# Edge-gated graph layer: a float32r expansion of two exact parts, masks and a subtraction on GpSimd, and lists built between edge tiles

## Chip, cores and metric

One core of a Trainium2 chip. The metric is the device time of one execution in microseconds (us), as a median over several. The profile shows one execution: TensorE (PE, with PEld for its weight loads), VectorE (DVE), ScalarE (ACT), GpSimd (POOL) and SyncE (SP, which only issues DMAs here). A ratio of two kernels is the mean time of one kernel's runs over the mean of the other's runs of the same rounds, so it is not quite the ratio of the medians that are quoted.

## The reference

16 batches, 1024 nodes, 256 features, everything in fp32. The adjacency matrix has some 9 entries in a column, so only these edges are worked on.

```
pre_u = x @ W1[:256];  pre_v = x @ W1[256:]
S[b,u,v] = sigmoid(relu(pre_u[b,u] + pre_v[b,v] + b1) @ W2 + b2)      # one gate per edge
a[b,v]   = sum_u S[b,u,v] * A[u,v] * x[b,u]
m[b,v]   = (sum_u A[u,v] * x[b,u]) * x[b,v]
z        = beta1*x + beta2*(a @ Wa + ba) + beta3*(m @ Wm + bm)
```

## The kernel before

The batches go in 4 **groups** of 4. A **block** is 128 target nodes of one group: 8 blocks to a group, 32 in all. Each block has two **windows** of 64 nodes, each window 640 edge slots in five **edge steps** of 128. `lists` makes, once per 128 nodes, which slot holds which edge. `rows` makes pre_u (written to a table in HBM) and pre_v (`pv`, kept in SBUF) for the next group.

```python
# lists(vt), its end: edge values fetched, then the masks (64 columns per edge step)
for j in range(TW):                      # 5 indirect DMAs for each of two windows
    nc.gpsimd.indirect_dma_start(out=val[:, i, j:j + 1], in_=adj_flat, in_offset=... vidx ...)
for j in range(TW):
    nc.vector.tensor_scalar(whose[:, i, j, :], place, L[:, j, 4:5], val[:, i, j:j + 1],
                            ALU.is_equal, ALU.mult)

# edges(g, vt, pv): one edge step j of window w
f = fetched[n % NF]                      # NF = 5 buffers
nc.gpsimd.indirect_dma_start(out=f, in_=table[g], in_offset=... uidx[:, i, j:j + 1] ...)
pc = psc.tile([P, 2, 2 * D], FP)         # PSUM, two buffers: the expansion of pre_v to slots
for h in range(2):
    q = (w + h) % 2 * W
    nc.tensor.matmul(pc[:, h, :], mark[q:q + W, j * P:(j + 1) * P], pv[q:q + W, h, :], ...)
nc.vector.tensor_tensor(t, f[:, :GD], pc, ALU.add)
for b in range(GB):                      # relu, times W2, summed: one score per edge and batch
    nc.vector.scalar_tensor_tensor(t[:, b, :], t[:, b, :], 0.0, w2_b, ALU.max, ALU.mult, accum_out=sc[:, b:b + 1])
nc.scalar.activation(gt, sc, AF.Sigmoid, bias=b2_b)
left = wk.tile([P, GB, 2, W], FP, name="left")            # three buffers
nc.scalar.activation(left[:, :, w, :], whose[:, i, j, :] (4 times), AF.Copy)         # ungated half
for b in range(GB):
    nc.scalar.activation(left[:, b, 1 - w, :], whose[:, i, j, :], AF.Copy, scale=gt[:, b:b + 1])
for b in range(GB):
    nc.tensor.matmul(acc[:, b, :], left[:, b], f[:, GD + b * D:GD + (b + 1) * D], ...)  # accumulation

# the main program
copy_h(0)
for nt in range(NT):
    pvs.append(rows(0, nt))
    lists(nt)                            # all eight lists before the first edge
for g in range(NG):
    for vt in range(NT):
        edges(g, vt, now[vt])
        if g + 1 < NG: pvs.append(rows(g + 1, vt))
```

A scheduler puts these instructions in order on each engine; within an engine they then run strictly in that order.

Of the kernel before, what the change touches and what calls it, by code (L numbers as in the profile page):

```python
# [8 lines left out]
FP = mybir.dt.float32  # L9
I32 = mybir.dt.int32  # L10
# [3 lines left out]
P = 128  # L14
# [3 lines left out]
def kernel(  # L18
# [18 lines left out]
):  # L37

# [54 lines left out]
    w_a = load_weights(Wa, "w_a")  # L93
    w_m = load_weights(Wm, "w_m")
    bias = load_rows(bm, D, "bias")
    ba_b = load_rows(ba, D, "ba_b")
    be1 = load_rows(beta1, 1, "be1")
    be2 = load_rows(beta2, 1, "be2")
    be3 = load_rows(beta3, 1, "be3")
    nc.vector.tensor_scalar(ba_b, ba_b, be2, None, ALU.mult)  # L100
    nc.vector.scalar_tensor_tensor(bias, bias, be3, ba_b, ALU.mult, ALU.add)
    nc.vector.tensor_scalar(w_a, w_a, be2, None, ALU.mult)
    nc.vector.tensor_scalar(w_m, w_m, be3, None, ALU.mult)
# [21 lines left out]
    nc.vector.tensor_scalar(before, row_of.rearrange("p w t v -> p w (t v)"), row, None, ALU.is_gt)  # L125
    late = const.tile([P, 1], FP, name="late")
# [10 lines left out]
    whose = const.tile([P, NT * NW, TW, W], FP, name="whose")  # L137
    thr = const.tile([P, NT], FP, name="thr")
    rest = const.tile([P, NT], FP, name="rest")
    nc.vector.memset(val, 0.0)  # L140
# [4 lines left out]
    pvp = main.enter_context(tc.tile_pool(name="pvp", bufs=NT + 1))  # L145
    wk = main.enter_context(tc.tile_pool(name="wk", bufs=3))
# [8 lines left out]
    def lists(vt):  # L155
# [42 lines left out]
        for w in range(NW):  # L198
            i = vt * NW + w
            Rv = Rw[:, w * RC:(w + 1) * RC]  # L200
            first = Rw[:, NW * RC + w:NW * RC + w + 1]
            nc.vector.tensor_tensor(Rv[:, 0:1], Rv[:, 0:1], first, ALU.add)
            nc.vector.tensor_copy(Rv[:, 1:2], first)
            early = wk.tile([P, E], FP, name="early", bufs=1)
            nc.vector.tensor_scalar(early, slot, Rv[:, 0:1], None, ALU.is_lt)
            mark = big.tile([P, E], FP, name="mark")
            nc.vector.scalar_tensor_tensor(mark, slot, first, early, ALU.is_ge, ALU.mult)  # L207
            nc.sync.dma_start(who[i], mark)
            pe = small("pe")
            for j in range(TW):  # L210
                nc.tensor.matmul(pe[:, j * RC:(j + 1) * RC], mark[0:W, j * P:(j + 1) * P], Rv[0:W, :],  # L211
                                 start=True, stop=True)
            L = wk.tile([P, TW, RC], FP, name="L", bufs=2)
            nc.vector.tensor_copy(L, pe[:, :TW * RC].rearrange("p (j r) -> p j r", r=RC))
            s_of = wk.tile([P, TW], FP, name="s_of", bufs=2)
            nc.vector.tensor_tensor(s_of, slot_of, L[:, :, 1], ALU.subtract)
            eq = wk.tile([P, TW, S], FP, name="eq", bufs=2)
            nc.vector.tensor_tensor(eq, nth.unsqueeze(1).to_broadcast([P, TW, S]),
                                    s_of.unsqueeze(2).to_broadcast([P, TW, S]), ALU.is_equal)
            nc.vector.tensor_tensor(eq, eq, L[:, :, 5:], ALU.mult)  # L220
            k_of = wk.tile([P, TW], FP, name="k_of", bufs=2)
            nc.vector.tensor_reduce(k_of, eq, AX.X, ALU.add)  # L222
            nc.vector.tensor_scalar(uidx[:, i, :], k_of, -1.0, float(N), ALU.mult, ALU.add)
            nc.vector.tensor_tensor(k_of, L[:, :, 2], k_of, ALU.subtract)
            nc.vector.scalar_tensor_tensor(k_of, L[:, :, 3], -BIG, k_of, ALU.mult, ALU.add)
            nc.vector.tensor_scalar(vidx[:, i, :], k_of, BIG + N, None, ALU.add)
            for j in range(TW):
                nc.gpsimd.indirect_dma_start(  # L228
                    out=val[:, i, j:j + 1], out_offset=None, in_=adj_flat,
                    in_offset=bass.IndirectOffsetOnAxis(ap=vidx[:, i, j:j + 1], axis=0),  # L230
                    bounds_check=N * N - 1, oob_is_err=False)
            for j in range(TW):
                nc.vector.tensor_scalar(whose[:, i, j, :], place, L[:, j, 4:5], val[:, i, j:j + 1],
                                        ALU.is_equal, ALU.mult)




    def rows(g, nt):
        hT = big.tile([P, GB, DC, P], FP, name="hT")  # L240
        nc.sync.dma_start(hT.rearrange("p b c n -> p (b c) n"),
                          xT_rows[:, g * GB * DC:(g + 1) * GB * DC, nt * P:(nt + 1) * P])
        hs = wk.tile([P, 2, DC, P], FP, name="hs", bufs=2)
        for w in range(NW):
            nc.gpsimd.tensor_copy(hs[:, :, :, w * W:(w + 1) * W],
                                  hT[:, 2:4, :, (1 - w) * W:(2 - w) * W])
        tab = big.tile([P, GD], FP, name="tab")
        pv = pvp.tile([P, 2, 2 * D], FP, name="pv")
        for h in range(2):
            pu = small("pu")  # L250
            for bb in range(2):
                for c in range(DC):
                    nc.tensor.matmul(pu[:, bb * D:(bb + 1) * D], hT[:, 2 * h + bb, c, :], w_u[:, c, :],  # L253
                                     start=(c == 0), stop=(c == DC - 1))
            nc.scalar.copy(tab[:, 2 * h * D:(2 * h + 2) * D], pu)  # L255
            pp = small("pp")
            for bb in range(2):
                for c in range(DC):
                    left = hs[:, bb, c, :] if h else hT[:, bb, c, :]
                    nc.tensor.matmul(pp[:, bb * D:(bb + 1) * D], left, w_v[:, c, :],  # L260
                                     start=(c == 0), stop=(c == DC - 1))
            nc.vector.tensor_tensor(pv[:, h, :].rearrange("p (b d) -> p b d", b=2),  # L262
                                    pp.rearrange("p (b d) -> p b d", b=2),
                                    b1_b.unsqueeze(1).to_broadcast([P, 2, D]), ALU.add)
        nc.sync.dma_start(table[g][nt * P:(nt + 1) * P, :GD], tab)
        return pv

# [7 lines left out]
    for i in range(NF):  # L275
        t = gat.tile([P, 2 * GD], FP, name=f"fetched{i}")
        nc.vector.memset(t, 0.0)
# [3 lines left out]
    def edges(g, vt, pv):  # L281
# [3 lines left out]
        for w in range(NW):  # L285
            i = vt * NW + w
            mark = big.tile([P, E], FP, name="mark")
            nc.sync.dma_start(mark, who[i])
            acc = psa.tile([P, GB, D], FP, name="acc")
            for j in range(TW):  # L290
# [3 lines left out]
                gt = wk.tile([P, GB], FP, name="gt")  # L294
# [4 lines left out]
                pc = psc.tile([P, 2, 2 * D], FP, name="pc")  # L299
                for h in range(2):  # L300
                    q = (w + h) % 2 * W
                    nc.tensor.matmul(pc[:, h, :], mark[q:q + W, j * P:(j + 1) * P], pv[q:q + W, h, :],  # L302
                                     start=True, stop=True)
                t = big.tile([P, GB, D], FP, name="t")
                nc.vector.tensor_tensor(t, f[:, :GD].rearrange("p (b d) -> p b d", b=GB),  # L305
                                        pc.rearrange("p h (b d) -> p (h b) d", b=2), ALU.add)
                sc = wk.tile([P, GB], FP, name="sc")
                for b in range(GB):
                    nc.vector.scalar_tensor_tensor(t[:, b, :], t[:, b, :], 0.0, w2_b,  # L309
                                                   ALU.max, ALU.mult, accum_out=sc[:, b:b + 1])  # L310

                nc.scalar.activation(gt, sc, AF.Sigmoid, bias=b2_b)  # L312
                left = wk.tile([P, GB, 2, W], FP, name="left")
                nc.scalar.activation(left[:, :, w, :], whose[:, i, j, :].unsqueeze(1).to_broadcast([P, GB, W]), AF.Copy)  # L314
                for b in range(GB):
                    nc.scalar.activation(left[:, b, 1 - w, :], whose[:, i, j, :], AF.Copy, scale=gt[:, b:b + 1])  # L316
                for b in range(GB):
                    nc.tensor.matmul(acc[:, b, :], left[:, b].rearrange("p k v -> p (k v)"),  # L318
                                     f[:, GD + b * D:GD + (b + 1) * D],
                                     start=(j == 0 and b % 2 == 0), stop=(j == TW - 1), skip_group_check=True)  # L320
            ev = big.tile([P, GB, D], FP, name="ev")
# [3 lines left out]
            for q in range(2):  # L325
# [6 lines left out]
                nc.scalar.copy(LT[:, q * 4:q * 4 + 4, 1, w * W:(w + 1) * W], src[:, :, a0:a0 + W])  # L332
        z = big.tile([P, GB, D], FP, name="z")
# [12 lines left out]

    copy_h(0)
    pvs = []
    for nt in range(NT):
        pvs.append(rows(0, nt))  # L350
        lists(nt)
    for g in range(NG):
        if g + 1 < NG:
            copy_h(g + 1)
        now, pvs = pvs, []
        for vt in range(NT):
            edges(g, vt, now[vt])
            if g + 1 < NG:
                pvs.append(rows(g + 1, vt))
    main.close()  # L360


    longest = const.tile([P, NT], FP, name="longest")
    nc.gpsimd.partition_all_reduce(longest, rest, P, bass_isa.ReduceOp.max)
    most = const.tile([P, 1], FP, name="most")
    nc.vector.tensor_reduce(most, longest, AX.X, ALU.max)
    turns = const.tile([P, NT + 1], I32, name="turns")
    nc.vector.tensor_copy(turns[:, :NT], longest)
    nc.vector.tensor_copy(turns[:, NT:], most)
# [109 lines left out]
```

## Time and profile before

| | before |
|---|---|
| median | 1948.74 us (1943.71 to 1953.58, 3 runs; with a fourth, 1949.91) |
| first store of z | 327.7 us |
| block in groups 0, 1, 2 / in group 3 | 51.8 / 45.5 us |
| boundary between groups | 67.2 us |
| busy: TensorE / VectorE / GpSimd | 82% / 61% / 23% |

The rows on blocks are read from the timeline of the SyncE queue: each store of z ends one block, so the distance of two stores is a block, and the distance from the last store of a group to the first of the next is a boundary. Groups of instructions have the columns: line, engine, operation, shape, count | busy us, mean ns | idle us before it, what ended most of it.

```profile
L295 POOL DMA_INDIRECT fetched<-table,uidx x320 | 326.3, 1020 | 1195.4 <-PE acc L318 982.4
L309 DVE SCALAR_TENSOR_TENSOR t<-t,w_b 128x256 f32<-128x256 f32 x1280 | 471.2, 423 | 18.4 <-DVE t L305 0.5
```

GpSimd has almost nothing but the gathers to do, and waits in front of them for the accumulation that frees a buffer. A multiply takes 423 ns.

### The profile page before, as it was taken

The numbers are of one execution on the slowest core, as the hardware profiler recorded it, in microseconds if no ns is written. First come the engines' busy times: TensorE is split into PE (matmuls) and PEld (weight loads), VectorE is DVE, ScalarE is ACT, GpSimd is POOL, SyncE is SP. The second block draws the span as 40 slices with busy tenths as digits, with TensorE's granted clock in tenths as the row PEclk, the third lists the DMA queues.
The fourth block names the chain that finished last, engine by engine and source line by source line (L and its number), as shares of the span: only waits on it lengthen the run. The fifth ranks groups of instructions, "written<-read, shape, count | busy, mean of one in ns | idle before, by whom it ended". The sixth has DMA issues, their size and how long they took to land. (4 is left out here: it accounts for less than half of the span.)

```text
span 1944.6 us, 22106 instructions
## 1 busy us (share of the span) xinstructions
PE 1590.1 (82%) x6640; PEld 1116.4 (57%) x6640; DVE 1193.9 (61%) x3595; ACT 726.4 (37%) x2306; POOL 442.1 (23%) x479
## 2 busy tenths in 40 slices
PE   1456459998888879999888879999998878989996
PEld 1345436666666646666666646666666645566664
DVE  4566666766666546566666456565566456766664
ACT  0000014444444324444444334344444334454443
POOL 0243352122222121221222122212221121222220
PEclk9676579999999989999999989999999989999999
DMA  9722247666666466666666466666666376666662
GB/s 273 244 86 83 69 156 263 208 242 245 240 248 248 144 228 223 216 235 224 233 245 238 152 241 242 237 224 221 228 230 232 130 267 245 244 238 235 227 236 98
DMA packets 151809, 414.09 MB, mean 213 GB/s; under 512 B 16656, under 2 KB 100112, under 8 KB 115472
## 3 DMA queue, kind: packets, MB, share of 16 engines
q0 software_dynamic: 48640, 296.70, 42.7%
q1 hardware_dynamic: 100800, 114.31, 17.4%
q10 hardware_dynamic: 2240, 1.58, 0.4%
q8 instruction: 55, 0.90, 0.2%
q14 instruction: 74, 0.61, 0.1%
HBM read 412.66 MB, written 55.57 MB: 241 GB/s over the span
## 5 line engine op out<-in xcount | busy, mean ns | idle before, releaser
L318 PE MATMUL acc<-fetched,left 128*128 128x256 f32 x2560 | 623.1, 394 | 78.8 <-ACT left L316 78.0
L318 PEld LDWEIGHTS acc<-fetched,left 128*128 128x128 f32 x2560 | 483.0, 195 | 248.5 <-ACT left L316 179.0
L295 POOL DMA_INDIRECT fetched<-table,uidx x320 | 326.3, 1020 | 1195.4 <-PE acc L318 982.4
L305 DVE TENSOR_TENSOR t<-fetched,pc 128x1024 f32<-128x1024 f32 x320 | 383.5, 1216 | 318.0 <-PE pc L302 285.9
L309 DVE SCALAR_TENSOR_TENSOR t<-t,w_b 128x256 f32<-128x256 f32 x1280 | 471.2, 423 | 18.4 <-DVE t L305 0.5
L302 PE MATMUL pc<-pv,mark 64*128 64x512 f32 x1280 | 404.2, 636 | 66.3 <-DVE t L305 59.7
L316 ACT ACTIVATE left<-whose,gt 128x64 f32<-128x64 f32 x1280 | 347.6, 339 | 9.5
L302 PEld LDWEIGHTS pc<-pv,mark 64*128 64x128 f32 x1280 | 130.3, 189 | 246.9 <-issue 119.7
L314 ACT ACTIVATE left<-whose 128x256 f32<-128x256 f32 x320 | 132.6, 414 | 367.4 <-PE acc L318 351.5
L312 ACT ACTIVATE gt<-sc,b_b 128x4 f32<-128x4 f32 x320 | 94.3, 295 | 322.1 <-DVE t L309 289.5
L255 ACT COPY tab<-misc 128x512 f32<-128x512 f32 x64 | 37.4, 585 | 400.4 <-PE misc L253 400.4
L253 PE MATMUL misc<-w_u,hT 128*128 128x256 f32 x512 | 135.7, 413 | 24.4 <-DMA hT<-in_xT_dram 24.4
L341 PE MATMUL misc<-w_m,LT 128*128 128x256 f32 x512 | 138.5, 394 | 1.7 <-ACT LT L332 0.3
L343 DVE TENSOR_TENSOR z<-misc,z 128x512 f32<-128x512 f32 x64 | 44.3, 692 | 153.5 <-PE misc L341 153.5
L341 PE MATMUL misc<-w_a,LT 128*128 128x256 f32 x512 | 132.7, 382 | 0.0
L253 PEld LDWEIGHTS misc<-w_u,hT 128*128 128x128 f32 x512 | 105.3, 208 | 40.6 <-DMA h_blk<-in_adjT_dram 24.4
L329 PEld LDWEIGHTS misc<-ident,ev 128*128 128x128 f32 x512 | 55.8, 142 | 103.3 <-ACT ev L324 103.3
L262 DVE TENSOR_TENSOR pv<-misc,b_b 128x512 f32<-128x512 f32 x64 | 44.1, 689 | 114.8 <-PE misc L260 113.3
L211 PE MATMUL misc<-Rw,mark 64*128 64x29 f32 x160 | 36.9, 391 | 94.4 <-DVE mark L207 63.5
L329 PE MATMUL misc<-ident,ev 128*128 128x128 f32 x512 | 71.4, 283 | 52.1 <-ACT ev L324 52.1
L341 PEld LDWEIGHTS misc<-w_m,LT 128*128 128x128 f32 x512 | 96.6, 194 | 25.2 <-ACT LT L332 13.1
L228 POOL DMA_INDIRECT val<-in_adjT_dram,vidx x80 | 84.7, 1059 | 114.2 <-DVE k_of L222 78.5
(84 smaller groups left out, 989.4 us busy)
## 6 DMA issues: line engine op xcount, KB each, us to landing
mark<-who SPq DMA_DIRECT2D x64, 320.0 KB
table<-in_x_dram SPq DMA_DIRECT2D x4, 4096.0 KB
hT<-in_xT_dram SPq DMA_DIRECT2D x32, 512.0 KB
table<-tab SPq DMA_DIRECT2D x32, 512.0 KB
h_blk<-in_x_dram SPq DMA_DIRECT2D x32, 512.0 KB
out_dram<-z SPq DMA_DIRECT2D x32, 512.0 KB
who<-mark SPq DMA_DIRECT2D x16, 320.0 KB
fetched<-table,uidx POOLq DMA_INDIRECT x320
```

Source lines behind the costliest of these rows:

```text
L228: nc.gpsimd.indirect_dma_start(out=val[:, i, j:j + 1], out_offset=None, in_=adj_flat, in_offset=bass.IndirectOffsetOnAxis(ap=vidx[:, i, j: ...
L253: nc.tensor.matmul(pu[:, bb * D:(bb + 1) * D], hT[:, 2 * h + bb, c, :], w_u[:, c, :], start=(c == 0), stop=(c == DC - 1))
L295: nc.gpsimd.indirect_dma_start(out=f, out_offset=None, in_=table[g], in_offset=bass.IndirectOffsetOnAxis(ap=uidx[:, i, j:j + 1], axis=0), ...
L302: nc.tensor.matmul(pc[:, h, :], mark[q:q + W, j * P:(j + 1) * P], pv[q:q + W, h, :], start=True, stop=True)
L305: nc.vector.tensor_tensor(t, f[:, :GD].rearrange("p (b d) -> p b d", b=GB), pc.rearrange("p h (b d) -> p (h b) d", b=2), ALU.add)
L309: nc.vector.scalar_tensor_tensor(t[:, b, :], t[:, b, :], 0.0, w2_b, ALU.max, ALU.mult, accum_out=sc[:, b:b + 1])
L312: nc.scalar.activation(gt, sc, AF.Sigmoid, bias=b2_b)
L314: nc.scalar.activation(left[:, :, w, :], whose[:, i, j, :].unsqueeze(1).to_broadcast([P, GB, W]), AF.Copy)
L316: nc.scalar.activation(left[:, b, 1 - w, :], whose[:, i, j, :], AF.Copy, scale=gt[:, b:b + 1])
L318: nc.tensor.matmul(acc[:, b, :], left[:, b].rearrange("p k v -> p (k v)"), f[:, GD + b * D:GD + (b + 1) * D], start=(j == 0 and b % 2 == 0 ...
L329: nc.tensor.transpose(pt[:, k * P:(k + 1) * P], ev[:, b, c * P:(c + 1) * P], ident)
L341: nc.tensor.matmul(pz[:, bb * D:(bb + 1) * D], LT[:, b * DC + c, k, :], wt[:, c, :], start=(k == 0 and c == 0), stop=(k == 1 and c == DC - 1))
```

## The change

Intent: (1) replace the fp32 expansion, four half-height instructions per edge step, by two float32r ones of full height; so that the rounding to float32r loses nothing, `pv` is split into a rounded part and the exact rest, one in each half of the 128 rows; (2) let GpSimd share the work: it builds the ungated half of `left`, and does the split's subtraction; (3) put each accumulation one step behind its expansion; (4) let edges start early: only list 0 is built ahead, the others between the two windows of group 0's blocks; (5) load some constants later, and move the test for left-over edges.

```diff
+    def split(pv):
+        for w in range(NW):
+            s = slice(w * W, (w + 1) * W)
+            nc.scalar.copy(X[s, w, :], pv[s])                                  # X is float32r
+            nc.gpsimd.tensor_tensor(low[s], pv[s], X[s, w, :].bitcast(FP), ALU.subtract)
+        for h in range(2):
+            nc.tensor.matmul(pl, swap, low[:, k], start=True, stop=True)       # to the other 64 rows
+            ...  nc.scalar.copy(X[s, w, k], pl[s])
@@ lists
-            for j in range(TW):
-                nc.vector.tensor_scalar(whose[:, i, j, :], place, L[:, j, 4:5], val[:, i, j:j + 1], ...)
+            nc.vector.tensor_copy(whom[:, i, :], L[:, :, 4])
@@ edges, one step
+                nc.gpsimd.tensor_scalar(left[:, :, w, :], place (4 times), whom[:, i, j:j + 1],
+                                        val[:, i, j:j + 1], ALU.is_equal, ALU.mult)
-                for h in range(2):
-                    nc.tensor.matmul(pc[:, h, :], mark[q:q + W, j * P:(j + 1) * P], pv[q:q + W, h, :], ...)
+                for h in range(2):
+                    nc.tensor.matmul(pc[:, k], mark[:, j * P:(j + 1) * P], X[:, w, k], ...)   # float32r
-                nc.scalar.activation(left[:, :, w, :], whose[:, i, j, :] (4 times), AF.Copy)
-                    nc.scalar.activation(left[:, b, 1 - w, :], whose[:, i, j, :], AF.Copy, scale=gt[:, b:b + 1])
+                    nc.scalar.activation(left[:, b, 1 - w, :], left[:, b, w, :], AF.Copy, scale=gt[:, b:b + 1])
@@ edges, the loop over steps
+            for j in range(TW):
+                new = front(j)
+                if last: back(j - 1, *last)      # accumulation of the step before
+                last = new
@@ edges, after the first window
+                if g == 0 and vt + 1 < NT: lists(vt + 1)
+                if vt + 1 < NT: cuts.append(split(now[vt + 1]))
@@ main
-    for nt in range(NT):
-        pvs.append(rows(0, nt))
-        lists(nt)
+    lists(0)
+    pvs = [rows(0, nt) for nt in range(NT)]
```

Cut away: the rows' copy `hs` (no longer needed), the late loads, the end test, the copy of the next group's rows of x into the table (now issued in a group's second block, not at its start), types and buffers. The masks `whose` of all windows are no longer kept; `left` is built from `whom` and `val`.

## The prediction

> **What bounds the kernel now.** I first read the page: which engine is busiest, and what the costly groups wait for.
>
> ```profile
> PE 1590.1 (82%) x6640; PEld 1116.4 (57%) x6640; DVE 1193.9 (61%) x3595; ACT 726.4 (37%) x2306; POOL 442.1 (23%) x479
> L318 PE MATMUL acc<-fetched,left 128*128 128x256 f32 x2560 | 623.1, 394 | 78.8 <-ACT left L316 78.0
> L305 DVE TENSOR_TENSOR t<-fetched,pc 128x1024 f32<-128x1024 f32 x320 | 383.5, 1216 | 318.0 <-PE pc L302 285.9
> L302 PE MATMUL pc<-pv,mark 64*128 64x512 f32 x1280 | 404.2, 636 | 66.3 <-DVE t L305 59.7
> L245 POOL COPY hs<-hT 128x256 f32<-128x256 f32 x64 | 27.5, 445 | 136.9 <-DMA hT<-in_xT_dram 136.6
> ```
>
> TensorE leads, but two waits face each other: VectorE's add waits 286 us for the expansion `pc`, and `pc` waits 60 us for the add that frees its PSUM buffer. Then the timeline of the SyncE queue: the stores of z mark the end of each block (128 nodes, 4 batches).
>
> ```profile
> 966.02 0.39 SPq L345 DMA_DIRECT2D out_dram<-z  x1
> 1017.36 0.39 SPq L345 DMA_DIRECT2D out_dram<-z  x1
> ...
> 1757.42 0.39 SPq L345 DMA_DIRECT2D out_dram<-z  x1
> 1802.46 0.39 SPq L345 DMA_DIRECT2D out_dram<-z  x1
> ```
>
> A block takes 51.3 us; in the last group, which makes no rows for a next group, 45.0. The 6.3 us between them is nearly the 6.9 us of TensorE work that is missing, so TensorE's in-order queue sets the block. Third, the busy times by stretch (PE, PEld, DVE, ACT, POOL, then clock, DMA share, GB/s): one block, one block of the last group, a group boundary, and everything before the first edge step.
>
> ```profile
> 966.02:1017.36 51.34, 46.09 (x202) 32.59 (x201) 32.55 (x97) 22.58 (x72) 11.09 (x12) 1.00 0.65 235
> 1757.42:1802.46 45.04, 40.85 (x170) 27.38 (x169) 31.13 (x95) 21.30 (x70) 10.13 (x10) 0.96 0.69 247
> 690.61:758.01 67.40, 52.23 (x206) 33.70 (x205) 38.69 (x115) 25.36 (x82) 16.00 (x17) 0.90 0.70 253
> 0.00:277.80 277.80, 124.33 (x502) 108.71 (x504) 161.56 (x496) 13.06 (x21) 93.96 (x113) 0.69 0.48 152
> ```
>
> A boundary costs 16 us more than a block: the next group's first gather waits for its last table rows. The first 277.8 us do no edge at all. Last, TensorE's timeline inside one block:
>
> ```profile
> 991.74 7.07 PE L318 MATMUL acc<-fetched,left 128*128 128x256 f32 x32
> 998.74 1.99 PE L302 MATMUL pc<-pv,mark 64*128 64x512 f32 x8
> 1001.19 1.13 PE L302 MATMUL pc<-pv,mark 64*128 64x512 f32 x4 [0.47 <-DVE t L305]
> 1003.48 1.99 PE L318 MATMUL acc<-fetched,left 128*128 128x256 f32 x8 [1.16 <-ACT left L316]
> 1005.40 1.98 PE L302 MATMUL pc<-pv,mark 64*128 64x512 f32 x6
> 1007.83 1.09 PE L329 MATMUL misc<-ident,ev 128*128 128x128 f32 x8 [0.45 <-ACT ev L324]
> ```
>
> 32 instructions in 7.00 us (991.74 to 998.74) is 0.216 to 0.219 us per instruction of 256 columns; each written fp32 product is two of them. The half-height products overlap in pairs: four instructions of 512 columns take some 0.86 us; six, an odd half alone, 1.7 to 1.9. After a burst of 32, VectorE has starved, and TensorE then waits for it and for ScalarE: ping-pong.
>
> **What the Trainium skill says.** (1) "FP8 and Floating Point Precision", TensorE Precision Notes: true fp32 takes four passes, reduced-precision fp32 truncates to FP22, which I read as one pass. The trace agrees on four: two instructions of 256 columns at 0.216 us are four times 256 columns at 2.4 GHz. It holds no float32r product. (2) "TensorE: Matmul & The Clock Gate", Back-to-back issue gap: 518 cycles for 512 columns, 0.216 us at 2.4 GHz; the trace shows this only as 2 x 256. (3) "GPSIMD Engine Reference", 3.1: two-input elementwise work costs about 2.6 cycles per element at 1.2 GHz. The trace has only a one-input copy, 445 ns for 256 elements. (4) "SBUF — State Buffer", SBUF: two separate sides: VectorE and GpSimd lock a shared port pair, also when VectorE has two SBUF inputs and GpSimd reads SBUF. The trace fits: the copy ranges from 386 to 596 ns, and the 420 ns multiply of L309 reaches 622.
>
> **The change, part by part, per block.** TensorE before: accumulation 80 instructions x 0.216 = 17.3; expansion 20 products, summed over one block's bursts, 10.2; products with Wm and Wa 32 x 0.216 = 6.9; rows of the next group 6.9; transposes 1.9. Sum 43.2, so 8.1 of the 51.3 us are waits.
>
> *Expansion.* 20 float32r products of full height x 0.216 = 4.3 us, plus two swap products 0.4, in place of 10.2: TensorE needs 37.7, 5.5 less. The odd unpaired halves vanish.
>
> *The split pays for it.* ScalarE gains two copies of 64x1024 at 1.0 (L324's row) and four of 64x512 at about 0.58 (L255's), 4.3 us, and loses ten L314 at 0.41: even. But its copies stand in the queue between a sigmoid and the accumulation that waits for it. GpSimd gains ten `left` builds of 128x256 at about 0.45 (hs copy), two subtractions of 64x1024 at an estimated 2.2 (skill, 3.1), and loses two hs copies: from 11 to about 19 us of 48, no bound. Through the port lock it can cost VectorE at most 10 x 0.4 + 2 x 2.2 us; I take 2 to 3. The built program's waits show that once a block the second subtraction waits for all outstanding gathers; it stands before the next block's gathers, while TensorE does z and rows, so I count it hidden.
>
> *New balance.* An edge step costs VectorE 1.14 + 4 x 0.35 = 2.5 us; it cost TensorE 1.73 + 1.02 and now costs 1.73 + 0.43 = 2.16. So within edge steps VectorE becomes the limiter, while in z and rows (13.8 us) two `pc` buffers let it run only three steps ahead, and it idles some 5 us. I followed the built order through a block: about 2.2 us of wait at the end of each of the two windows (accumulation, ev, transposes), 2 us behind VectorE after the rows, 1 behind ScalarE's copies, 2 for the port lock, 1 for late gathers, 1.5 for hand-offs: 9.8. Block: 37.7 + 9.8 = 47.5, in the last group without rows 41.5.
>
> *Lists.* Before, the first add is at 277.8. In the built order only list 0 precedes the rows. But the copies of x still fill the DMA queues (share 0.99 until 80 us), and the third hT load is behind them. Then six rows x 6.9 = 41, landing of the last table rows 4.8, first gather 6.0 (both as at 696.8 to 707.6): first add at 132, 146 us earlier. The seven other lists come back inside group 0: some 18 us of VectorE work each and two round trips to TensorE, in order before the second window's adds, so both engines' edge work stands still for some 20 us; the ten small gathers (13 us of GpSimd, 1.3 each) then stand before the next block's. With 2 us of lost hiding less 5 us of TensorE waits filled, a block with a list is 65. What is gained at the start, 146, is given back by 7 x 17.5 = 122.
>
> *Late loads, end test.* Constants ready earlier than they are used, and a few us after the last store: 2 to 3 us at most.
>
> *Sum.* First block's store at 132 + 60 (five steps 15, list 22, five steps 16, z 7) = 192; six list blocks 390 and one of 47.5: 629. Groups 1 and 2: 63.5 + 7 x 47.5 = 396 each: 1421. Group 3: 57.5 + 7 x 41.5 = 348: 1769. From the last store to the end 8: 1777; the timed runs lie a few us above the profiled span: **1780 us**, 8.7% less.
>
> **The rivals.** A: VectorE takes over as the bound and is slowed by GpSimd's lock, with the waits handed from `pc` to VectorE's sums. For it: 32.6 us of VectorE in a block plus up to 8.4 of lock plus the idle of the row phase is 46 to 48 already. Then a block stays at 50 and the total near 1860. B: the split's waits are hidden and the new order (one accumulation behind one expansion, no bursts of 32) ends the ping-pong. For it: the starving after each burst, 4.8 to 5.1 us twice a block. Against it: two `pc` buffers remain. A block then takes 43, and with lists of 58 the total is near 1650. C: float32r is not one pass, or drains the array on each change of type. With two passes the expansion takes 8.6, hardly less than 10.2, and only rounding of the odd halves and the start is left: about 1880. D: the lists simply move; group 0 then takes 70 a block and eats the start's whole gain: 1810. Gathers are no rival of weight: the DMA share would rise from 0.65 to about 0.71.
>
> **Range and chances.** A, C and D set the upper end, 1880; B and shorter lists the lower, 1680. To miss 2% (1910) two of A, C and D would have to hold at once. Faster 0.92, same 0.06, slower 0.02.
>
> **What would show it.** In the profile after: expansion products near 0.216 us apart back to back, half as many instructions; stores of z 47 to 48 us apart in groups 1 and 2, 41 to 42 in group 3, 65 in group 0; first add near 132; VectorE's wait for `pc` well under 286 us; GpSimd `left` near 0.45 us and subtraction near 2.2. The prediction is wrong if stores stay 50 apart (A or C; the product's duration tells which), or if VectorE's multiplies are longer on average than 423 ns by over 10% (A), or if group 0's blocks are under 58 or over 70.

## The result, and the profile after

The changed kernel takes **2052.97 us** (2039.69 to 2057.08, 4 runs) against 1949.91 (1943.71 to 1953.58, 4 runs) on the same chip: ratio 1.052, interval 1.046 to 1.058. Slower by 5%, where 1780 us were predicted. The result is correct. First the page, engine totals and groups.

```profile
PE 1507.7 (73%) x6064; PEld 1201.1 (58%) x6064; DVE 1259.2 (61%) x3526; ACT 741.3 (36%) x2178; POOL 1047.9 (51%) x806
L307 POOL TENSOR_SCALAR left<-place,whom,val 128x256 f32<-128x256 f32 x320 | 446.0, 1395 | 482.1 <-PE acc L328 449.5
L314 DVE TENSOR_TENSOR t<-fetched,pc 128x1024 f32<-128x1024 f32 x320 | 387.7, 1217 | 342.4 <-DMA fetched<-table,uidx 222.1
L318 DVE SCALAR_TENSOR_TENSOR t<-t,w_b 128x256 f32<-128x256 f32 x1280 | 550.8, 486 | 20.1
L301 POOL DMA_INDIRECT fetched<-table,uidx x320 | 354.6, 1108 | 63.5 <-issue 45.9
L312 PE MATMUL pc<-X,mark 128*128 128x512 f32 x640 | 257.5, 496 | 109.5 <-DVE t L314 103.5
L264 POOL TENSOR_TENSOR low<-pv,X 64x1024 fp32r<-64x1024 f32 x64 | 151.5, 2367 | 259.2 <-DMA fetched<-table,uidx 92.7
```

TensorE did lose what it was to lose: 1590 us busy became 1508, with half as many expansion instructions. But VectorE's add, which waited 286 us for `pc` before, now waits 222 us for the gathers (98 us for `pc` are left in its list of waits). GpSimd went from 442 to 1048 us busy. That a product costs what was predicted, TensorE's timeline shows:

```profile
1799.77 0.81 PE L312 MATMUL pc<-X,mark 128*128 128x512 f32 x2
1800.42 1.89 PE L328 MATMUL acc<-fetched,left 128*128 128x256 f32 x8
1801.96 1.27 PE L312 MATMUL pc<-X,mark 128*128 128x512 f32 x4
```

From 1799.77 to 1801.96 two products and eight accumulation instructions start: 2.19 us for ten, 0.219 each. A product alone takes a little more: where products follow one another at full clock and without a wait, the trace has them 0.224 to 0.236 us apart (median 0.231), the accumulation instructions 0.216.

The busy times by stretch (from one store of z to the next; PE, PEld, DVE, ACT, POOL, then clock, DMA share, GB/s) of a block of group 2 and a block of group 3:

```profile
1359.95:1411.18 51.23, 43.13 (x184) 34.58 (x183) 35.52 (x97) 22.89 (x68) 29.19 (x22) 0.93 0.64 233
1797.86:1852.05 54.19, 38.25 (x152) 29.75 (x151) 35.66 (x95) 21.88 (x66) 30.27 (x22) 0.87 0.56 201
```

A block still takes 51.2 us, and in group 3, where TensorE's rows fall away, 50.3 on average instead of 45.5: TensorE no longer sets the pace. GpSimd is busy 29 to 30 us of a block, not 11 as before and not the 19 predicted. No engine is full (TensorE, the busiest, is at 84% in group 2).

The clock in these lines is lower than before, and no run here was made to test it. The trace records only full and half speed; at half speed the accumulation instructions start 0.427 us apart, not 0.216. The mean granted clock of the whole run fell from 0.930 to 0.867: some 550 us at half speed instead of 270, with TensorE busy in 374 of them instead of 143. Work at half speed takes twice as long, so up to 115 us of TensorE time (an estimate, half of the difference) may belong to it. Whether that is a cause of the loss or follows from the waits stays open. It is not needed for a loss of this size: one run below is as slow at a clock of 0.920.

What a busy share cannot show, GpSimd's timeline at the start of a window does:

```profile
1798.61 1.22 POOL L307 TENSOR_SCALAR left<-place,whom,val 128x256 f32<-128x256 f32 x1 [11.70 <-PE acc L328]
1800.00 1.09 POOL L301 DMA_INDIRECT fetched<-table,uidx  x1 [0.17 <-issue]
1801.14 1.23 POOL L307 TENSOR_SCALAR left<-place,whom,val 128x256 f32<-128x256 f32 x1
1802.55 1.45 POOL L301 DMA_INDIRECT fetched<-table,uidx  x1 [0.18 <-PE acc L328]
```

Builds and gathers alternate in one queue; the third build, at 1804.05, stands in the chain below. A build starts 2.5 to 2.9 us after the build before it, so GpSimd now needs as long for an edge step as VectorE (2.5 us by the prediction's count), in a burst that can start only when an accumulation frees a buffer (11.7 us waited). The chain of work goes through exactly these pieces, ending in a gather:

```profile
1804.05 1.49 POOL left L307
...
1805.72 7.55 DMA fetched<-table,uidx
...
1813.39 1.23 DVE t L314
```

The other GpSimd step shows in VectorE's multiplies, a few microseconds later:

```profile
1822.21 4.84 POOL L264 TENSOR_TENSOR low<-pv,X 64x1024 fp32r<-64x1024 f32 x2 [8.25 <-PE misc L268]
```
```profile
1822.44 2.40 DVE L318 SCALAR_TENSOR_TENSOR t<-t,w_b 128x256 f32<-128x256 f32 x1
1824.77 2.56 DVE L318 SCALAR_TENSOR_TENSOR t<-t,w_b 128x256 f32<-128x256 f32 x1
```

While GpSimd subtracts twice, two multiplies take 2.40 and 2.56 us, where the median is 0.42. That looks like the lock; the run with the subtraction on VectorE, below, tests it.

Where the 277 us between the predicted last store (1769) and the measured one (2046.5) lie, from the stores:

| part | predicted | measured | difference |
|---|---|---|---|
| first store | 192 | 221.4 | +29 |
| group 0, 7 blocks | 437.5 | 513.9 | +76 |
| three boundaries | 184.5 | 234.0 | +50 |
| groups 1 and 2, 14 blocks | 665 | 725.4 | +60 |
| group 3, 7 blocks | 290.5 | 351.8 | +61 |

### The profile page after: what moved, and what is told of

Same layout as the page of the kernel before. It is cut to its first block, busy times and chain, and to the rows that moved or that the text cites. A ratio compares the mean times of both kernels' runs of the same rounds, so it can differ in the third digit from the quotient of the medians. Undisturbed runs are those within 1.5% of the kernel's fastest.

```text
span 2054.5 us, 21673 instructions
## 1 busy us (share of the span) xinstructions
PE 1507.7 (73%) x6064; PEld 1201.1 (58%) x6064; DVE 1259.2 (61%) x3526; ACT 741.3 (36%) x2178; POOL 1047.9 (51%) x806
## 4 chain that ended last, share of the span: by engine, by line
PE 29%; DMA 11%; issue 9%; POOL 7%; DVE 7%; ACT 5%; POOLq 0%; DVEq 0%; ACTq 0%
DMA fetched<-table,uidx 11%; PE acc L328 10%; PE misc L361 9%; POOL left L307 4%; PE misc L347 3%; DVE t L318 3%; PE misc L248 3%; PE misc L242 3%; DVE t L314 2%; ACT ev L342 2%; POOL fetched L301 2%; ACT left L323 2%; DVE ev L341 1%; POOL low L264 1%; ACT X L271 1%
## 5 line engine op out<-in xcount | busy, mean ns | idle before, releaser
L328 PE MATMUL acc<-fetched,left 128*128 128x256 f32 x2560 | 681.7, 414 | 149.4 <-ACT left L323 147.6
L307 POOL TENSOR_SCALAR left<-place,whom,val 128x256 f32<-128x256 f32 x320 | 446.0, 1395 | 482.1 <-PE acc L328 449.5
L328 PEld LDWEIGHTS acc<-fetched,left 128*128 128x128 f32 x2560 | 512.0, 207 | 282.7 <-ACT left L323 211.0
L318 DVE SCALAR_TENSOR_TENSOR t<-t,w_b 128x256 f32<-128x256 f32 x1280 | 550.8, 486 | 20.1
L301 POOL DMA_INDIRECT fetched<-table,uidx x320 | 354.6, 1108 | 63.5 <-issue 45.9
L323 ACT ACTIVATE left<-left,gt 128x64 f32<-128x64 f32 x1280 | 342.8, 338 | 54.3 <-POOL left L307 31.4
L312 PE MATMUL pc<-X,mark 128*128 128x512 f32 x640 | 257.5, 496 | 109.5 <-DVE t L314 103.5
L264 POOL TENSOR_TENSOR low<-pv,X 64x1024 fp32r<-64x1024 f32 x64 | 151.5, 2367 | 259.2 <-DMA fetched<-table,uidx 92.7
L347 PE MATMUL misc<-ident,ev 128*128 128x128 f32 x512 | 101.1, 362 | 168.0 <-ACT ev L342 168.0
L312 PEld LDWEIGHTS pc<-X,mark 128*128 128x128 f32 x640 | 123.1, 206 | 171.1 <-DVE t L314 141.9
L248 PE MATMUL misc<-w_v,hT 128*128 128x256 f32 x512 | 121.9, 381 | 0.0
```

Of the source, the lines that this page charges most:

```text
L248: nc.tensor.matmul(pp[:, bb * D:(bb + 1) * D], hT[:, 2 * h + bb, c, :], w_v[:, c, :], start=(c == 0), stop=(c == DC - 1))
L264: nc.gpsimd.tensor_tensor(low[s], pv[s], X[s, w, :].bitcast(FP), ALU.subtract)
L301: nc.gpsimd.indirect_dma_start(out=f, out_offset=None, in_=table[g], in_offset=bass.IndirectOffsetOnAxis(ap=uidx[:, i, j:j + 1], axis=0), ...
L307: nc.gpsimd.tensor_scalar(left[:, :, w, :], place.unsqueeze(1).to_broadcast([P, GB, W]), whom[:, i, j:j + 1], val[:, i, j:j + 1], ALU.is_e ...
L312: nc.tensor.matmul(pc[:, k], mark[:, j * P:(j + 1) * P], X[:, w, k], start=True, stop=True)
L323: nc.scalar.activation(left[:, b, 1 - w, :], left[:, b, w, :], AF.Copy, scale=gt[:, b:b + 1])
```

## The experiments

Theory after the comparison: three parts of the change each cost more than was counted. **Q**: the builds of `left` in GpSimd's queue hold back the gathers. **L**: the subtraction on GpSimd locks VectorE and waits for gathers. **O**: lists between the windows cost far more than at the start. The rival to all of them, **V**: VectorE is the bound at some 50 us a block, once the expansion is short. Every run is of 4 executions, and correct unless said. They ran on two chips, on which the kernel before took the same time within 0.3%. "Changed" is the changed kernel.

### One part undone at a time

**Builds of `left` undone.** Masks per window, made by GpSimd (128x64, five per window), and ScalarE copies again:

```diff
+            for j in range(TW):
+                nc.gpsimd.tensor_scalar(whose[:, j, :], place, whom[:, i, j:j + 1], val[:, i, j:j + 1], ...)
-                nc.gpsimd.tensor_scalar(left[:, :, w, :], place (4 times), whom..., val..., ...)
+                nc.scalar.activation(left[:, :, w, :], whose[:, j, :] (4 times), AF.Copy)
```

> The changed kernel, but left's ungated half is again a ScalarE copy; GpSimd only makes a 128x64 table slice per step, once per window, which waits for no accumulation. Theory Q (GpSimd's in-order queue: a left build of 1.23 us, held until an accumulation frees its buffer, stands before each gather): in groups 1 and 2 blocks fall from 51.8 us to 46 to 48, in group 3 from 50.3 to 42 to 44, boundaries from 78 to about 68, VectorE's wait for gathers from 222 us to under 80; total 1850 to 1900. Theory L (port lock by the two subtractions) or theory O (new order and lists are the loss): blocks stay at 50 or more, total 2000 or more.

Measured 2006.46 us, ratio to before 1.029 (1.026 to 1.031): 46 us better, far less than theory Q wanted; by its total it fits the other theories. Boundaries fell from 78 to 68.6 to 70.0, blocks only to 50.0. Multiplies still averaged 482 ns, and the add still waited 176 us for gathers.

**Subtraction undone**, on VectorE instead:

```diff
-            nc.gpsimd.tensor_tensor(low[s], pv[s], X[s, w, :].bitcast(FP), ALU.subtract)
+            nc.vector.tensor_tensor(low[s], pv[s], X[s, w, :].bitcast(FP), ALU.subtract)
```

> The changed kernel with the subtraction that makes low on VectorE instead of GpSimd. Theory L (a 2.4 us GpSimd subtraction locks VectorE out and waits for all gathers): VectorE's multiplies fall back from a mean of 486 ns to under 440, blocks in groups 1 and 2 to 49 or less, total 1960 or less. Theory Q: multiplies shorten too, but VectorE takes on 2 x 1.2 us a block and the gathers stay late: blocks 50 to 51.5, total 2000 to 2040.

2014.64 us, ratio 1.033 (1.031 to 1.036): 38 us better. The multiplies went back to 428 ns, so the lock was the subtraction's; the total is the one that theory Q expected of this run. But blocks stayed at 51.7 to 52.0.

**Lists undone**, all eight between the rows at the start:

```diff
-    lists(0)
-    pvs = [rows(0, nt) for nt in range(NT)]
+    for nt in range(NT):
+        pvs.append(rows(0, nt))
+        lists(nt)
```

> The changed kernel with all lists made at the start between the rows, as before the change. If the moved lists are the whole loss (theory O), the total falls to 1950 or under. My account: first add back at about 275, group 0's blocks from 73.4 us to about 53, so the store of the last block of group 0 at about 695 instead of 735; groups 1 to 3 unchanged; total about 2010.

1969.5 us, ratio 1.009 (1.005 to 1.013): 83 us better, between the two expectations. By the stores: the first comes 66 us later, group 0's seven blocks are 141 us shorter.

**The builds of `left` put into the kernel before**, where all else stays:

> The kernel before, with only one thing added: left's ungated half is built by GpSimd (128x256 compare and multiply) instead of copied by ScalarE. Theory Q: blocks of groups 1 and 2 rise from 51.8 us (mean with rows) to 54 to 57, boundaries from 67.4 to 74 or more, total 2010 to 2080, VectorE's wait for gathers from 30 us to over 100. Theories L and O: under 1% from before, as neither the subtraction nor the order is in it.

2046.61 us, ratio 1.052 (1.047 to 1.058). This one part alone makes the old kernel as slow as the whole change does. A build took 1398 ns there too; blocks of groups 1 and 2 grew from 51.8 to 55. The wait for gathers rose from 30 to 86 us, less than the 100 that theory Q expected.

### Parts undone together

> The changed kernel with both new GpSimd steps moved off it at once: the ungated half of left is again a ScalarE copy, and the subtraction of the split is on VectorE. Lists stay between the windows of group 0. Theory Q+L (GpSimd's queue holds back the gathers through the left builds, and its subtraction locks VectorE and waits for gathers; each one, undone alone, leaves the other in charge, so the two gains add up to more than 46 + 38 us): blocks of groups 1 and 2 at 46 to 49 us, of group 3 at 42 to 45, boundaries under 70, blocks with a list still 70 to 74, total 1880 to 1950. Rival V (VectorE itself is the bound once the expansion is short, so that neither matters much): blocks stay at 50 to 51, total 1970 to 2000.

1938.63 us, ratio 0.994 (0.990 to 0.999). The two moves together give 114 us, where alone they gave 46 and 38. Blocks of groups 1 and 2 are 48.2 and 46.9, of group 3 44.5. Rival V falls.

> As the run with both GpSimd steps moved, and all lists made at the start between the rows, as before the change. What is left of the change is the float32r expansion of two exact parts, the new order of accumulation behind expansion, and the late loads. If the lists cost 70 to 85 us between the windows, as the run with only the lists moved says, this runs at 1810 to 1870 by theory Q+L, and beats both kernels; by rival V (VectorE is the bound at 50 us a block) it runs at 1890 to 1930. First store at 290 to 330, blocks of group 0 at 48 to 52.

**1800.11 us** (1798.93 to 1803.31), ratio 0.924 (0.922 to 0.926): 7.6% faster than the kernel before, and a little below the expected range. What is left of the change in it is the float32r expansion with its split (subtraction on VectorE), the new order, masks taken out of the lists (now per window, on GpSimd), and the moved loads and copies. Its stores and its multiplies:

```profile
914.82 0.39 SPq L368 DMA_DIRECT2D out_dram<-z  x1
960.82 0.39 SPq L368 DMA_DIRECT2D out_dram<-z  x1
```
```profile
L317 DVE TENSOR_TENSOR t<-fetched,pc 128x1024 f32<-128x1024 f32 x320 | 387.9, 1216 | 166.3 <-PE pc L315 76.1
L321 DVE SCALAR_TENSOR_TENSOR t<-t,w_b 128x256 f32<-128x256 f32 x1280 | 472.5, 424 | 12.2
```

Blocks of groups 1 and 2 average 46.8 and 48.1 us: the 47.5 of the prediction. The add's waits are half of what either other kernel has.

**The new order undone** in that version (each accumulation right behind its own expansion):

> The kernel with all three undone, but each accumulation stands right behind its own expansion, as in the kernel before, and not one step later. If the new order is what lets VectorE and TensorE overlap, a block gets 3 to 6 us longer (50 to 53 us in groups 1 and 2) and the total 100 to 180 us longer. If the scheduler or the two expansion buffers decide the overlap anyway, it stays within 1.5% of the kernel with the new order.

1855.64 us, ratio 0.954 (0.951 to 0.957): 55 us slower than with the new order, between the two expectations. So the order is worth 3%. Blocks with rows take 51.0, hardly less than the 51.8 of the kernel before, although the expansion has half the instructions: there the shorter expansion shows only together with the order. In group 3 the old order is better (42.9 against 44.7), which I did not follow up.

### What each part costs by itself

As the gains did not add, two runs put one part back into the fast version.

> The fast version (lists first, subtraction on VectorE, 1800 us) with left again built by GpSimd per edge step, as in the change. The same move cost the kernel before 5.2%. Theory Q (left builds of 1.2 us stand between the gathers and wait for free buffers): 70 to 120 us longer, 1870 to 1920, boundaries 71 to 79, VectorE waits much longer for gathers. If the left builds matter only together with the subtraction there: within 25 us.

1936.78 us, ratio 0.992 (0.987 to 0.997): +137 us for the builds of `left`, above the expected range.

```profile
L307 POOL TENSOR_SCALAR left<-place,whom,val 128x256 f32<-128x256 f32 x320 | 448.5, 1402 | 739.8 <-PE acc L328 700.2
L314 DVE TENSOR_TENSOR t<-fetched,pc 128x1024 f32<-128x1024 f32 x320 | 389.1, 1217 | 251.3 <-DMA fetched<-table,uidx 117.8
L318 DVE SCALAR_TENSOR_TENSOR t<-t,w_b 128x256 f32<-128x256 f32 x1280 | 479.6, 429 | 16.9
```

The multiplies are hardly longer (429 ns), so this is not VectorE locked out. The builds are: those that overlap a multiply in time took 1.55 us on average, the others 1.23. By the waits, the loss comes through GpSimd's queue, in which builds wait 700 us for accumulations; the add's wait for gathers is 118 us, against 67 in the fast version. Whether order, length or buffers make it is not separated.

> The fast version with only the subtraction back on GpSimd. Theory L (it locks VectorE out of its port for about 2 us twice a block and stands ahead of the next block's gathers): 60 to 110 us longer, 1860 to 1910, blocks 49.5 to 50.5, boundaries near 69, VectorE multiplies at 470 to 490 ns on average. If it hurts only in company of the left builds: within 25 us.

1879.84 us, ratio 0.964 (0.959 to 0.968): +80 us for the subtraction, with multiplies at 500 ns (the profiled run is the slowest of the four, 1898.18):

```profile
L321 DVE SCALAR_TENSOR_TENSOR t<-t,w_b 128x256 f32<-128x256 f32 x1280 | 568.1, 500 | 17.8 <-DVE t L317 0.5
L317 DVE TENSOR_TENSOR t<-fetched,pc 128x1024 f32<-128x1024 f32 x320 | 387.9, 1217 | 265.3 <-DMA fetched<-table,uidx 123.0
```

The multiplies take 95 us more than in the fast version (568.1 to 472.5), but that is not the loss itself: VectorE is rid of the 64 subtractions, which took it 1.22 us each, and is busy only 21 us longer in all (1262.5 to 1241.7). What grew is its waiting: the add waits 265.3 us instead of 166.3, and 123.0 of it instead of 66.9 for gathers. The run does not separate the lock from the subtraction's place in GpSimd's queue.

The version with lists between the windows (1938.63) gives +138 for these. The three sum to 355 us; the changed kernel is 253 above the fast version. So they overlap; I read it as each shortening the time in which another would be waited for.

**Only the order of GpSimd's queue**: the changed kernel with a window's five gathers written ahead of its five builds.

> The changed kernel whole, but each window's five row gathers stand ahead of its five left builds in the program (a gather then waits only for the accumulation that frees its buffer, not for a left build that waits for an accumulation). If the order of GpSimd's queue is what the left builds cost, 20 to 60 us shorter: 1990 to 2035, boundaries from 78 to 68 to 72. If their duration or the lock is what counts, within 0.7% of the changed kernel (2053).

2097.56 us, ratio 1.077 (1.072 to 1.081), a miss for both theories: it got 2.4% slower than the changed kernel. The scheduler followed the wish only in part (a build still stands before each of the first two gathers), and now ScalarE waited 151.6 us for builds, in place of 31.4. But the multiplies also grew, from 486 to 520 ns, 46 us in all, and the clock fell to 0.839. So the run does not show that the order is the cost of the builds; what the best order would give stays open.

### The lists

**Moved in the kernel before:**

> The kernel before, with only its lists moved between the windows of group 0's edge tiles. By the run of the changed kernel with lists first, the move costs 75 us or so net: total 2000 to 2040, blocks of group 0 at 71 to 76 us, first store near 210 to 230. If instead the move hurts only because GpSimd is full in the changed kernel (11 of 51 us busy here), the lists cost 15 to 18 us a block as predicted, and the total stays within 20 us of the kernel before: 1930 to 1970.

2062.84 us, ratio 1.058 (1.056 to 1.060): +115 us, more than either theory said. Blocks with a list take 87 us, 35 more than others, although GpSimd has no builds and no subtraction there. So O does not come from the other parts.

One list in the version with both GpSimd steps moved (blocks with a list 80, others 48). VectorE first, then GpSimd:

```profile
389.01 1.22 DVE L160 TENSOR_TENSOR t<-t,ukey 128x1024 f32<-128x1024 f32 x1
...
413.03 0.17 DVE L223 TENSOR_SCALAR vidx<-k_of 128x5 int32<-128x5 f32 x1
413.11 2.35 DVE L317 TENSOR_TENSOR t<-fetched,pc 128x1024 f32<-128x1024 f32 x2
...
436.34 1.22 DVE L317 TENSOR_TENSOR t<-fetched,pc 128x1024 f32<-128x1024 f32 x1 [6.58 <-DMA fetched<-table,uidx]
```
```profile
412.74 1.00 POOL L225 DMA_INDIRECT val<-in_adjT_dram,vidx  x1 [19.06 <-DVE uidx L220]
...
425.75 4.37 POOL L298 TENSOR_SCALAR whose<-place,whom,val 128x64 f32<-128x64 f32 x5
430.27 1.10 POOL L305 DMA_INDIRECT fetched<-table,uidx  x1 [0.16 <-issue]
```

VectorE does no edge step from 389.0 to 413.1, 24 us; then ten small gathers hold GpSimd for 13 us, five masks for 4.4, and only then come the next block's row gathers, for which VectorE waits 6.6 us.

**Row gathers ahead of the small ones:**

> The kernel with both GpSimd steps moved off and the lists still between the windows (1939 us, list blocks 78 to 81 us, 33 more than the others), with one change of order: each window issues its five gathers of table rows first, and in group 0 the five small gathers of adjacency values of that window after them, just before the masks that need them. Theory G (of the 33 us that a list costs, about 13 to 17 are the ten small gathers of 1.3 us each, which stand in GpSimd's queue ahead of the next block's row gathers; the rest is VectorE's work, which is in order): list blocks fall to 64 to 69 us, total 1840 to 1870. Rival R (VectorE's and TensorE's list work sets the block, and the small gathers lie beside it): list blocks stay at 75 or more, total above 1905.

1935.15 us, ratio 0.991 (0.986 to 0.996), blocks with a list 79.5 to 82.9: nothing gained. But the test failed as a test: its trace shows the ten small gathers still ahead of the row gathers, because the scheduler did not keep the written order.

**Small gathers left out** (result wrong, all values 1):

```diff
-                nc.gpsimd.indirect_dma_start(out=val[:, i, j:j + 1], ..., in_=adj_flat, ...)
-    nc.gpsimd.memset(val, 0.0)
+    nc.gpsimd.memset(val, 1.0)
```

> The same kernel with the small gathers of adjacency values left out and the values set to 1: a WRONG result on purpose. It takes the ten small gathers off GpSimd's queue and off the DMA queues, and leaves all of the lists' VectorE and TensorE work. Theory G: list blocks at 62 to 67 us and a total of 1830 to 1855, near the kernel with the small gathers moved behind. Rival R: list blocks at 75 or more, total above 1905.

1878.33 us, ratio 0.960 (0.956 to 0.964): between the two theories. Group 0's seven blocks took 483.1 us, against 531.9 with the small gathers and 338.3 with lists first. Six of these seven blocks make a list. So of the 32.3 us that a list adds to a block here, 8.1 are the small gathers and 24.1 VectorE's and TensorE's list work.

**Masks out of the lists, in the kernel before:**

```diff
-            for j in range(TW):
-                nc.vector.tensor_scalar(whose[:, i, j, :], place, L[:, j, 4:5], val[:, i, j:j + 1], ...)
+            nc.vector.tensor_copy(whom[:, i, :], L[:, :, 4])
@@ edges, each window
+            for j in range(TW):
+                nc.gpsimd.tensor_scalar(whose[:, j, :], place, whom[:, i, j:j + 1], val[:, i, j:j + 1], ...)
```

> The kernel before, with only this part of the change: the masks of the edges are no longer made by VectorE inside the lists, where VectorE waits 37 us in all for the small gathers, but per window by GpSimd (128x64 each); ScalarE copies them as before. If this wait is what holds the start, the first store comes 35 to 55 us earlier (from 328 to 275 to 290), blocks stay at 51 to 53, and the total is 1895 to 1920. If the start is set by the loads, the rows or the lists' own work, the first store stays within 10 us and the total within 0.7%, or gets worse by the masks on GpSimd.

1914.53 us, ratio 0.980 (0.977 to 0.983): faster, but whether by 2% is unclear. The first store comes at 287.4 instead of 327.7. In the kernel before, VectorE stood in its own queue waiting for the small gathers:

```profile
DVE whose L233 <- DMA val<-in_adjT_dram,vidx: 36.6, 32, 3.1
```

(36.6 us in all, 32 times.) So 40 us of the late start came from the masks and not from where the lists stand.

### A still faster version

The fast version with each window's row gathers ahead of its five masks:

> The fastest kernel so far (lists first, both steps off GpSimd; 1800 us) with each window's five row gathers issued ahead of its five masks, which take 3.6 us of GpSimd. If the gathers' wait behind the masks still matters (VectorE's add waits 58 us in all for gathers there or more), it gains 10 to 40 us: 1760 to 1790. If each gather waits for a free buffer anyway, nothing: within 0.5%.

**1786.61 us** (1782.52 to 1801.54), ratio 0.918 (0.912 to 0.923), the best. Its interval touches that of the fast version (0.922 to 0.926, another set of rounds), so the last 0.7% are likely, not shown.

### All runs in one table

Columns: median, ratio to the kernel before, and from the stores of the profiled run: first store of z, blocks of group 0 that make a list (all of group 0's seven, where the lists come first), blocks of group 1, of group 3, first boundary.

| kernel | us | ratio | first store | group 0 | group 1 | group 3 | boundary |
|---|---|---|---|---|---|---|---|
| before | 1949.91 | 1 | 327.7 | 51.8 | 51.9 | 45.5 | 67.4 |
| changed | 2052.97 | 1.052 | 221.4 | 77.3 | 51.8 | 50.3 | 78.1 |
| changed, `left` undone | 2006.46 | 1.029 | 221.6 | 80.1 | 50.0 | 48.6 | 68.6 |
| changed, subtraction undone | 2014.64 | 1.033 | 219.5 | 78.0 | 52.0 | 47.5 | 72.7 |
| changed, lists undone | 1969.5 | 1.009 | 287.0 | 53.2 | 50.8 | 50.3 | 78.0 |
| changed, gathers ahead of builds | 2097.56 | 1.077 | 220.2 | 79.7 | 54.7 | 47.8 | 78.5 |
| `left` and subtraction undone | 1938.63 | 0.994 | 215.8 | 80.7 | 48.2 | 44.5 | 65.8 |
| the same, small gathers last | 1935.15 | 0.991 | 215.1 | 81.3 | 47.7 | 43.9 | 66.2 |
| the same, no small gathers (wrong result) | 1878.33 | 0.960 | 209.9 | 72.4 | 47.7 | 44.1 | 68.2 |
| all three undone (fast version) | 1800.11 | 0.924 | 276.2 | 48.3 | 46.8 | 44.7 | 67.3 |
| fast version, `left` put back | 1936.78 | 0.992 | 279.1 | 52.6 | 51.9 | 48.2 | 73.7 |
| fast version, subtraction put back | 1879.84 | 0.964 | 277.7 | 50.7 | 49.8 | 48.9 | 71.7 |
| fast version, old order | 1855.64 | 0.954 | 274.3 | 50.7 | 51.0 | 42.9 | 65.4 |
| fast version, gathers ahead of masks | 1786.61 | 0.918 | 274.9 | 47.3 | 47.3 | 44.7 | 65.5 |
| before, builds of `left` put in | 2046.61 | 1.052 | 329.8 | 54.1 | 55.1 | 48.4 | 71.7 |
| before, lists between | 2062.84 | 1.058 | 225.3 | 87.1 | 52.2 | 45.8 | 67.0 |
| before, masks per window | 1914.53 | 0.980 | 287.4 | 53.2 | 51.8 | 45.8 | 67.2 |

## Why the prediction was wrong, step by step

- **Bound before: argued, not shown.** The prediction took TensorE's queue to set the block, as group 3's blocks, which make no rows, are shorter by as much. One run speaks against so plain a bound: with the short expansion in the old order, a block with rows is only 0.8 us shorter (51.0), though the split's own work is in it too.
- **Expansion: right.** 640 float32r products in place of 1280. They start 0.231 us apart (predicted 0.216), where two passes would be 0.43. Rival C is out.
- **Block of 47.5 us: right for a kernel that was not the one predicted, and partly by luck.** With both GpSimd steps moved off it, blocks are 46.8 and 48.1, and 44.7 in group 3 (41.5 predicted). But the waits that the prediction lists add up to 11.9 us, not 9.8: the 2.2 us stand for each of two windows and were counted once. Its own terms gave 49.6.
- **The step that failed: "GpSimd gains ten `left` builds of 128x256 at about 0.45 (hs copy) ... from 11 to about 19 us of 48, no bound".** A build took 1.23 us at the median and 1.40 on average, three times the copy from which it was sized. And no share of 48 was the right measure: builds and gathers are one in-order queue, 2.5 to 2.9 us per edge step in a burst, as much as VectorE needs, behind three `left` buffers. Cost by itself: 137 us. That the move costs so much is shown, both ways; that it does so through the queue is read from the waits, and the run on the queue's order did not confirm it. Late gathers were put at 1 us a block; the add waited 222 us for them in all.
- **Port lock: mechanism and size right, the wait beside it wrong.** "I take 2 to 3" us a block out of up to 8.4. The multiplies took 550.8 us instead of 471.2, 2.5 us for each of 32 blocks, and 3.0 in the fast version with the subtraction put back. But there it cost 80 us, with VectorE busy only 21 us longer and the add waiting 99 us longer. So that the second subtraction's wait for all gathers is "hidden" was probably wrong: in the changed kernel subtractions waited 92.7 us for gathers, in the queue in front of the next ones. How much of the 80 us this is was not separated.
- **Lists: "a block with a list is 65".** Measured 75 to 77 in five blocks and 85 in a sixth. The start gained 135 us for the first add (142.6, predicted 132), but the first store only 106. The prediction set 146 won against 122 lost. Of the 106 won, 40 came with the masks' removal alone; moving the lists won only 60 to 66 (two pairs of runs), and lost 141 in the changed kernel and 194 without its GpSimd work. Three terms were missing or too small: the small gathers, 8 us a list, which the prediction named and then did not add; the list's in-order work, 24 us net where 17 was used for everything (both sizes from the version without the GpSimd work; in the changed kernel a list adds 23.5 in all); and the question of what the start would be with the lists left where they were.
- **Boundaries, 63.5 predicted, 78 measured.** With `left` back on ScalarE they are 69, with everything undone 66. So some 9 of these 14 us are the builds.
- **New order.** Not valued by itself in the prediction, only as rival B, whose blocks of 43 us came in no group with rows; it is worth 55 us in the fast version.
- **Rivals.** A (VectorE bound and lock, 1860) named the right neighbour, and all three signs of being wrong came: stores 51.8 us apart, multiplies 15% longer, blocks with a list over 70. But GpSimd's builds cost as much as the lists, and no rival named them. D (lists merely move, 1810) was too kind.

**Open:** the best order of builds and gathers in GpSimd's queue, the split of the subtraction's 80 us into lock and wait, what the half-speed clock costs, what the late loads and the moved copy of x are worth, and the excess of the first block (79 us from first add to first store, 60 predicted), which I have not taken apart.

## What to carry to other kernels

Size an operation that moves to another engine by that operation on that engine, and where an engine issues the transfers that others wait for, add up its queue per step of the loop, with the gathers in it, instead of a share of its time. Undo the parts of a change together as well as one at a time: here two undone alone gave 46 and 38 us, together 114. And before work is moved from a prologue into a loop, ask how short the prologue gets by a smaller step: 40 us of it went by not waiting in the wrong queue.

## What the Trainium skill lacked or had wrong

- "GPSIMD Engine Reference", 4.1 Engine selection, calls one-input work on GpSimd "roughly line-rate". Here a compare-and-multiply with two per-partition scalars took 1232 ns at the median for 128x256, and 577 to 587 ns for 128x64; the same page's 3.1 was right for the two-input subtraction (2.2 us estimated, 2.37 measured for 1024 elements).
- "SBUF — State Buffer", SBUF: two separate sides, says that whichever side starts first holds the pair for the whole instruction and the other is blocked; the trace agrees for the subtraction: two multiplies of 2.40 and 2.56 us. It gives no size for short instructions in turn: with builds on GpSimd, the multiplies stayed at 429 ns on average, and the builds beside one grew from 1.23 to 1.55 us.
- No page that I read gives the rate of a float32r product: 0.224 to 0.236 us for 512 columns and 128 rows, where fp32 takes four instructions of 0.216 us for as many columns.
- No page that I read gives how long an indirect DMA holds GpSimd's queue: 1.02 to 1.16 us with 8 KB per index, and 1.03 to 1.13 us with 4 bytes, so a list's ten small gathers cost the queue as much as ten large ones.
